# Moving a chain of small steps one to six places later in a hand-written order: layer 1's sums' stage of a two-layer graph attention kernel

## The chip, the cores and the metric

The kernel runs on one core of a Trainium2 chip, as one program. The metric is device time in microseconds (us), from one launch to its end. Three runs of the kernel before took 2566.87, 2554.59 and 2565.46 us; the median is 2565.46 us.

The core has a matrix engine (TensorE, PE in the profile; its weight loads are listed apart as PEld), a vector engine (VectorE, DVE), an engine for activations and copies (ScalarE, ACT), a general engine that here issues the gathers (GpSimd, POOL), and an engine that issues plain transfers (SyncE, SP). Each works through its own list of instructions in order. One waits for another by semaphores. PE writes to an accumulator memory (PSUM); the other operands lie in the on-chip memory (SBUF).

## The reference, cut to what matters

Two layers of relational graph attention over 3125 nodes of 768 features and 53125 edges (both directions and the loops) of three types, then a residual sum and a layer norm:

```python
def rgat_conv(x, W, q, k, b, src, dst, etype, heads, out_ch, n_nodes):
    xr = jnp.einsum('nd,rdf->rnf', x, W)
    oi = xr[etype, dst]; oj = xr[etype, src]
    alpha = jax.nn.leaky_relu(oi @ q + oj @ k, 0.2)
    m = jax.ops.segment_max(alpha, dst, num_segments=n_nodes)
    e = jnp.exp(alpha - m[dst])
    z = jax.ops.segment_sum(e, dst, num_segments=n_nodes)
    a = e / (z[dst] + 1e-16)
    msg = (a[:, :, None] * oj.reshape(-1, heads, out_ch)).reshape(-1, heads * out_ch)
    return jax.ops.segment_sum(msg, dst, num_segments=n_nodes) + b

h = jax.nn.elu(rgat_conv(x, W1, q1, k1, b1, ..., heads=4, out_ch=192))
out = rgat_conv(h, W2, q2, k2, b2, ..., heads=1, out_ch=768)
return layernorm(x + out)
```

Edges are sorted by `dst`. So the edges that end in one block of 128 nodes are one run of at most 17 slots of 128 edges.

## The kernel before, in words

There are 25 blocks of 128 nodes, and three stages after the set-up. Stage 1 (`phase1`) makes the table `x W1` for all types, with the keys, queries and weights of the edges. Stage 2 (`phase2`, L933 to L1203) is the one that changes. Stage 3 (`phase3`) gathers and sums for layer 2 and writes the output.

In stage 2 every block goes through five kinds of work:

1. **Gathers.** `gather(k)` (the helper at L490) has POOL issue one indirect transfer: 128 rows of 772 floats from the table into one of 14 buffers (`share` and `g`, `NG` at L937). There are 17 for a block, 14 for block 0.
2. **Selections.** `high(k)` (L1001, helper L482) has DVE make four matrices, one a head, that hold the edges' weights at the node of each edge.
3. **Sums.** `sums(k)` (L1010, matmuls at L1028): PE adds the selected rows into the accumulator `acc`. The 17 slots are taken in two batches of 96 matmuls, 128x32 by 128x193. A batch is issued when its last slot has come up: the first with the 8th slot of the block, the second with the 17th. A gather's buffer is free again when the sums that read it are done.
4. **The chain from the sums to the next layer's input.** `e_y` on DVE (L1036, L1037, and four L1041: divide by the sum of the weights and add the bias, result `y`), `e_x` on ACT (L1047: `ey = exp(y)`), `e_h` on DVE (L1087, L1088: ELU, in `ey`), `e_t` on PE (L1095: six 128x128 transposes into `pt`), `e_s` on ACT (L1102: the high part of `hT`) and `e_s2` on DVE (L1108: the low part). `y`, `ey` and `pt` have one buffer each, `hT` two.
5. **The dense products.** `d_part` (L1125, matmuls L1121): `h W2` in 18 parts of about 4.5 matmuls each, 90 in all (72 with 512 columns and 18 with 262). They write five pieces of the result into `po`, which has two buffers: pieces 0 to 3 take 18 matmuls of 512 columns each, piece 4 takes 18 of 262. `d_row(b, p)` (L1133) empties piece p: DVE copies two short columns of piece 0 (L1140, L1141) and one column into a row's start (L1145), ACT copies the rest (L1148) into the rows `r`, and SP stores a finished row into the table of layer 2 (L1153). So piece p+2 can't start before ACT has copied piece p.

What sets the order is written out by hand: a loop over steps k, one a slot of 17 a block (427 steps up to the last sums), and a list `ev` of what else is issued at a step. In a step the order is: the gather of slot k, the late keys, the sums of slot k-5, the selections of slot k-3, then what `ev` holds, older blocks first. No scheduler moves anything after that, so each engine's list is in this order. For block b, step e is the step after that of its second batch of sums:

```python
            e = SLF + i * SL + LAG          # one step after the block's last sums
            if i > 0:
                for d, f in ((0, e_y), (1, e_x), (2, e_h), (3, e_t), (4, e_s), (4, e_s2)):
                    when(e + d, f, b)
            e += 6
            for m in range(6 * R):
                k = e + m * SL // (6 * R) if i else first + 5 + m * (SL + 3) // (6 * R)
                when(k, d_part, b, m)
```

The products of a block so run over 17 steps, under the sums of the next block, and end beside that block's own chain. Block 0 has a chain of its own (`e_first`) and spreads its 18 parts over 20 steps.

Two things more stand in this order. The last four blocks (`LATE`) get the weights of their edges in this stage: four key gathers on POOL a block (`key`, L953) for 17 blocks (1 to 17), at step e+8, and four times the steps `l_load` to `l_put` (L956 to L996), which use the tiles `y`, `ey` and `pt` between two chains. And at step 427, SP issues the loads of `x` for stage 3 (`x_load3`).

Of the kernel before, what the change touches and what calls it, by code (L numbers as in the profile page):

```python
# [37 lines left out]
SL = 17  # L38
# [22 lines left out]
def kernel(  # L61
# [21 lines left out]
    R = layers[0]["W"].shape[0]  # L83
# [376 lines left out]
    def base(b):  # L460

        return SLF + (b - 1) * SL if b else 0
# [470 lines left out]
    def phase2(work, psum, wH, wL):  # L933
# [226 lines left out]
        def when(k, f, *a):  # L1160
            ev.setdefault(k, []).append((f, a))

        LAG = 5
        first = SLF + LAG - 1
        for i, b in enumerate(order):
            e = SLF + i * SL + LAG
            if i > 0:
                for d, f in ((0, e_y), (1, e_x), (2, e_h), (3, e_t), (4, e_s), (4, e_s2)):
                    when(e + d, f, b)
            e += 6  # L1170
            for m in range(6 * R):
                k = e + m * SL // (6 * R) if i else first + 5 + m * (SL + 3) // (6 * R)
                when(k, d_part, b, m)
                for p, (f, n) in enumerate(PIECES):
                    if m < (f + n) * 6 * R / WW <= m + 1:
                        when(k + 1, d_row, b, p)
            when(e + 2 + SL, d_q, b)
        at_key = {base(2 + i // KEYS) + 13: keys[i // KEYS * KEYS:i // KEYS * KEYS + KEYS]
                  for i in range(0, len(keys), KEYS)}
        for i in range(LATE):  # L1180
            e = base(2 + (SL * (i + 1) - 1) // KEYS + 2) + LAG
            for d, f in ((5, l_load), (6, l_alpha), (7, l_max), (8, l_scan), (10, l_back), (11, l_put)):
                when(e + d, f, NB - LATE + i)
        for k in range(max(ev) + 1):
            if k < NK:
# [359 lines left out]
    with tc.manual_schedule():  # L1545
        with tc.tile_pool(name="share", bufs=1) as pool:
# [4 lines left out]
            with tc.tile_pool(name="wbuf", bufs=1) as wbuf:  # L1551
# [33 lines left out]
                with tc.tile_pool(name="work2", bufs=1) as work, tc.tile_pool(name="psum2", bufs=1, space=PSUM) as psum:  # L1585
                    phase2(work, psum, wH, wL)
# [540 lines left out]
```

## Time and profile before

| what | us | from |
|---|---|---|
| median of three runs | 2565.46 | times |
| profiled execution, its own time | 2581.38 | times |
| its span, first to last instruction | 2579.6 | profile |
| stage 2: first sums to last dense product | 812.5 to 1803.3 | timeline |
| 17 blocks with key gathers (1 to 17), from the end of block 1's sums to that of block 18's | 692.3, or 40.7 a block | timeline |
| 6 blocks without (18 to 23), to the end of block 24's sums | 210.6, or 35.1 a block | timeline |
| from the end of block 24's sums to the last product | 27.2 | timeline |

The span is that of one profiled execution, on the same program; its own time of 2581.38 us stands 15.9 us (0.6%) above the median of the three runs. A block's time is counted from the recorded end of its second batch of sums to that of the next block. In a row of the timeline the first number is the start in us, the second the time taken, then engine, line, operation, output and inputs; in brackets stands the engine's idle time before it and what ended it ("remote" and "issue": nothing that the profile shows).

### The profile page before, as it was taken

What the parts mean: (1) busy time and instruction counts of PE and PEld (TensorE: products, weight loads), DVE (VectorE), ACT (ScalarE), POOL (GpSimd) and SP (SyncE); (2) the same over time, 40 slices, a digit from 0 to 9 for tenths busy, and PEclk for the clock granted to TensorE, in tenths of its full rate; (3) what the DMA queues carried; (4) which work ended last, traced back from release to release, by engine and by line L of the source; (5) the groups of instructions that cost most, each with busy time, mean ns of one, the idle gap of its engine ahead of it and who ended that gap; (6) DMA issues with size and microseconds to landing.
All of it is one profiled execution on the core that took longest, in us unless ns stands there. A gap on an engine that the chain in (4) does not pass through costs nothing.

```text
span 2579.6 us, 40091 instructions
## 1 busy us (share of the span) xinstructions
PE 1916.1 (74%) x13939; PEld 1341.8 (52%) x13939; DVE 1198.0 (46%) x4331; ACT 383.7 (15%) x834; POOL 1347.9 (52%) x1326
## 2 busy tenths in 40 slices
PE   8958887888996888788888888989365554455555
PEld 8846676666775666565655656667022222222223
DVE  7423443433544545455454555563244444445444
ACT  6301111111110111101111111111011111111111
POOL 4355666555533454555555455441655566556551
PEclk9978898888998888898989989999566666667667
DMA  7633343443568665665656657665867777767772
GB/s 224 154 114 109 126 150 112 139 135 111 183 211 297 191 210 177 199 187 186 215 176 207 192 191 237 213 220 171 286 212 239 252 262 269 252 226 252 242 236 84
DMA packets 161766, 506.39 MB, mean 196 GB/s; under 512 B 48028, under 2 KB 57521, under 8 KB 161556
## 3 DMA queue, kind: packets, MB, share of 16 engines
q0 software_dynamic: 81936, 331.52, 41.5%
q1 hardware_dynamic: 69389, 157.78, 17.5%
q10 hardware_dynamic: 10230, 14.43, 1.7%
q8 instruction: 114, 1.87, 0.3%
q14 instruction: 97, 0.79, 0.1%
HBM read 412.74 MB, written 95.69 MB: 197 GB/s over the span
## 4 chain that ended last, share of the span: by engine, by line
PE 22%; another core or an unknown queue 18%; issue 15%; DVE 10%; POOL 6%; ACT 2%; DMA 1%; POOLq 0%; ACTq 0%; DVEq 0%; SPq 0%
PE po L1121 8%; POOL G L490 6%; DVE selp L482 5%; PE acc L1340 5%; PE po L742 4%; PE acc L1028 3%; DMA G<-ftab,ridx 1%; ACT r L1148 1%; DVE sT L1251 1%; PE pt L1095 1%; ACT hT L1102 1%; DVE y L1041 0%; ACT ey L1047 0%; DVE F L1299 0%
## 5 line engine op out<-in xcount | busy, mean ns | idle before, releaser
L1121 PE MATMUL po<-wH,hT 128*128 128x512 f32 (+1 forms) x1500 | 487.9, 409 | 61.1 <-ACT hT L1102 58.3
L490 POOL DMA_INDIRECT kt<-kt,ridx x374 | 396.6, 1060 | 248.2 <-issue 108.5
L490 POOL DMA_INDIRECT G<-ftab,ridx x374 | 377.9, 1010 | 276.3 <-PE acc L1340 115.9
L742 PE MATMUL po<-wH,xT 128*128 128x512 f32 (+1 forms) x1320 | 433.8, 404 | 39.1 <-ACT share L774 17.8
L1340 PE MATMUL acc<-G,selp 128*32 128x385 f32 (+1 forms) x2292 | 304.6, 637 | 165.6 <-issue 91.7
L482 DVE TENSOR_SCALAR selp<-frow,fdl,pall 128x32 f32<-128x32 f32 (+1 forms) x1688 | 376.3, 313 | 9.7 <-remote 9.7
L490 POOL DMA_INDIRECT share<-ftab,ridx x239 | 247.4, 1035 | 244.9 <-PE acc L1028 162.7
L1121 PEld LDWEIGHTS po<-wH,hT 128*128 128x128 f32 x1500 | 301.8, 212 | 135.1 <-ACT hT L1102 62.0
L742 PEld LDWEIGHTS po<-wH,xT 128*128 128x128 f32 x1320 | 258.6, 205 | 102.1 <-issue 30.2
L1121 PE MATMUL po<-wL,hT 128*128 128x512 f32 (+1 forms) x750 | 308.1, 411 | 0.0
L1340 PEld LDWEIGHTS acc<-G,selp 128*32 128x32 f32 x2292 | 128.1, 134 | 315.8 <-issue 194.6
L742 PE MATMUL po<-wL,xT 128*128 128x512 f32 (+1 forms) x660 | 260.2, 394 | 8.6 <-issue 8.1
L490 POOL DMA_INDIRECT g<-ftab,ridx x135 | 139.9, 1036 | 148.4 <-PE acc L1028 99.7
L1028 PE MATMUL acc<-share,selp 128*32 128x193 f32 x3088 | 198.9, 340 | 23.7 <-issue 14.1
L1148 ACT COPY r<-po 128x262 f32<-128x262 f32 (+5 forms) x175 | 71.8, 436 | 737.1 <-remote 391.0
L1121 PEld LDWEIGHTS po<-wL,hT 128*128 128x128 f32 x750 | 160.2, 214 | 33.9 <-issue 7.7
L1028 PEld LDWEIGHTS acc<-share,selp 128*32 128x32 f32 x3088 | 119.5, 113 | 89.2 <-issue 60.0
L742 PEld LDWEIGHTS po<-wL,xT 128*128 128x128 f32 x660 | 135.2, 205 | 34.3 <-issue 12.2
L1251 DVE TENSOR_SCALAR sT<-bc,cols 128x512 bf16<-128x512 f32 (+1 forms) x125 | 82.8, 662 | 94.5 <-PE bc L1245 91.8
L1028 PE MATMUL acc<-g,selp 128*32 128x193 f32 x1688 | 119.4, 334 | 5.7 <-issue 5.4
L1245 PE MATMUL bc<-d,one 1*128 1x512 bf16 (+1 forms) x125 | 49.4, 395 | 95.6 <-DVE sT L1251 67.3
L1271 DVE TENSOR_TENSOR oh<-oh,pq 128x153 f32<-128x153 f32 x25 | 7.9, 316 | 213.9 <-remote 200.6
(309 smaller groups left out, 2040.9 us busy)
## 6 DMA issues: line engine op xcount, KB each, us to landing
ftab<-r SPq DMA_DIRECT2D x74, 386.0 KB
ftab<-share SPq DMA_DIRECT2D x71, 386.0 KB
share<-in_L_gnn_W_dram SPq DMA_DIRECT2D x36, 384.0 KB
w_d<-w2hl SPq DMA_DIRECT2D x18, 768.0 KB
sT<-dr_d SPq DMA_DIRECT2D x25, 534.0 KB
share<-in_x_dram SPq DMA_DIRECT2D x27, 384.0 KB
xb_d<-share SPq DMA_DIRECT2D x25, 384.0 KB
xr<-in_x_dram SPq DMA_DIRECT2D x21, 384.0 KB
```

The source lines that it names most:

```text
L482: V.tensor_scalar(sel.rearrange("p (t f) -> p t f", f=32), of, dl[:, b, j:j + 1], p, op0=ALU.is_equal, op1=ALU.mult)
L490: return G.indirect_dma_start(out=to, out_offset=None, in_=tab, in_offset=_index(i[:, j:j + 1]), bounds_check=NP * R - 1, oob_is_err=False)
L742: m = T.matmul(po[:, :n], xT[:, s, t, :], w[:, t, KQ + f:KQ + f + n], start=(i == 0), stop=(i == 3 * DT - 1))
L1028: T.matmul(acc[32 * t:32 * t + 32, h // 2, c], sel[:, h, 32 * WINDOW[i].index(t):][:, :32], g[:, h * CW:(h + 1) * CW], start=(i == u[0] an ...
L1095: T.transpose(pt[:, t // 3, (t % 3) * P:(t % 3 + 1) * P], s["ey"][:, t * P:(t + 1) * P], ident)
L1102: S.copy(hT[:, 0], p3)
L1121: T.matmul(po[:, :n], hT[:, k, t, :], w[:, t, f:f + n], start=(i == 0), stop=(i == 3 * DT - 1))
L1148: S.copy(o[:, 1 + at - a:1 + at + m], po[:, got - a:got + m])
L1245: T.matmul(bc[:, :n], one, s["d"][:, 4 * i * P:4 * i * P + n], start=True, stop=True)
L1251: V.tensor_scalar(s["sT"][:, 4 * i * P:4 * i * P + n], bc[:, :n], cols[:, b:b + 1], None, op0=ALU.is_equal)
L1271: V.tensor_mul(oh, oh, s["pq"][:, :SL * R * 3].rearrange("p (j k) -> p j k", j=SL))
L1340: T.matmul(acc[32 * t:32 * t + 32, c, :HALF + c], st[b, j][:, 32 * WINDOW[j].index(t):][:, :32], gs[:, (base(b) + j) % NG, 1 + c * HALF:][ ...
```

## The change

The chain's steps move: `e_y`, `e_x` and `e_h` by one step, `e_t` by three, `e_s` and `e_s2` by four. The dense products of every block but block 0 move by six steps (and the `d_row` and `d_q` with them); block 0's keep their start and are spread over 26 steps. The late blocks' steps `l_load` to `l_put` move by two to five. What is computed, the buffers and the number of instructions stay the same.

```diff
             e = SLF + i * SL + LAG
             if i > 0:
-                for d, f in ((0, e_y), (1, e_x), (2, e_h), (3, e_t), (4, e_s), (4, e_s2)):
+                for d, f in ((1, e_y), (2, e_x), (3, e_h), (6, e_t), (8, e_s), (8, e_s2)):
                     when(e + d, f, b)
-            e += 6
+            e += 12
             for m in range(6 * R):
-                k = e + m * SL // (6 * R) if i else first + 5 + m * (SL + 3) // (6 * R)
+                k = e + m * SL // (6 * R) if i else first + 5 + m * (SL + 9) // (6 * R)
                 when(k, d_part, b, m)
...
-            for d, f in ((5, l_load), (6, l_alpha), (7, l_max), (8, l_scan), (10, l_back), (11, l_put)):
+            for d, f in ((8, l_load), (9, l_alpha), (9, l_max), (12, l_scan), (13, l_back), (16, l_put)):
                 when(e + d, f, NB - LATE + i)
```

In PE's list of a block this reads as follows. Before: second sums of block b, 23 matmuls of products of block b-1, the six transposes of b, the last 17 products of b-1, the first 10 of b, first sums of b+1, 40 products of b, second sums of b+1. After: second sums of b, 36 products of b-1, the transposes of b, first sums of b+1, the last 31 products of b-1 (13 of 512 columns and 18 of 262), the first 23 of b, second sums of b+1.

In ACT's list, before: the copy of piece 2 of block b-1, exp of b, piece 3, high part of `hT` of b, piece 4. After: the two copies of piece 1 of block b-1, exp of b, piece 2, high part of `hT` of b, piece 3, piece 4.

## The prediction

> **What bounds the kernel now.** First I read stage 2's share and the waits in it, then one block's timeline on PE, DVE, ACT and POOL. The waits name two stalls of PE, and both are in the chain that the change moves:
>
> ```profile
> PE pt L1095 <- DVE ey L1088: 63.2, 23, 3.0
> ...
> PE po L1121 <- ACT hT L1102: 58.3, 17, 5.0
> ```
>
> The first is the transposes' wait for `ey`, 2.75 us in each of 23 blocks; the second the next products' wait for `hT`, 3.4 us in 17 blocks. The table by stretches, from the end of block 1's sums to that of block 18's and of block 24's:
>
> ```profile
> 873.17:1565.43 692.26, 576.34 (x4909) 421.38 (x4909) 345.90 (x1486) 76.22 (x156) 367.89 (x358) 0.89 0.62 194
> 1565.43:1776.07 210.64, 190.25 (x1733) 144.95 (x1733) 119.32 (x512) 26.65 (x55) 97.48 (x95) 0.94 0.66 210
> ```
>
> Columns: time, then busy time of PE, PEld, DVE, ACT, POOL, the granted clock, DMA share, GB/s. PE is busy 83 and 90% of the time, no other engine over 57%, DMA 62 to 66%: PE sets the pace. Its clock is 0.89 and 0.94 of full speed; the difference to 1 is lost too. One block with key gathers:
>
> ```profile
> 1323.58 0.68 PE L1028 MATMUL acc<-share,selp 128*32 128x193 f32 x9 [0.21 <-issue]
> ...
> 1332.54 0.88 PE L1095 MATMUL pt<-fident,ey 128*128 128x128 f32 x6 [2.84 <-DVE ey L1088]
> ```
> ```profile
> 1327.43 0.16 DVE L1036 TENSOR_SCALAR rz<-acc 128x4 f32<-128x4 f32 x1 [6.07 <-remote]
> ...
> 1331.53 0.96 DVE L1088 SCALAR_TENSOR_TENSOR ey<-y,ey 128x768 f32<-128x768 f32 x1
> ```
> ```profile
> 1328.20 0.59 ACT L1148 COPY r<-po 128x512 f32<-128x512 f32 x1 [11.72 <-remote]
> 1329.35 0.84 ACT L1047 ACTIVATE ey<-y 128x768 f32<-128x768 f32 x1 [0.56 <-issue]
> 1335.49 0.66 ACT L1148 COPY r<-po 128x6 f32<-128x6 f32 x2 [5.29 <-remote]
> 1338.96 0.80 ACT L1102 CAST hT<-pt 128x768 fp32r<-128x768 f32 x1 [2.81 <-remote]
> ```
>
> Read them against each other. PE's sums end at 1324.26, but DVE sees them at 1327.43, 3.2 us later. The last matmul of piece 2 ends at 1325.39 and ACT's copy starts at 1328.20 (2.8 late); piece 3's ends at 1329.58 and its copy starts at 1335.49 (5.9 late); the transposes end at 1333.42 and `hT` starts at 1338.96 (5.5 late). Why PE's results arrive late isn't shown ("remote"), but it goes with POOL's runs of gathers. In this block POOL issues without a pause, the four keys last:
>
> ```profile
> 1323.84 1.00 POOL L490 DMA_INDIRECT share<-ftab,ridx  x1 [0.72 <-remote]
> ...
> 1337.58 1.00 POOL L490 DMA_INDIRECT kt<-kt,ridx  x1 [0.30 <-issue]
> ```
>
> `hT` comes 0.4 us after this run ends at 1338.58. In the first block without keys the run ends at 1574.55, and `hT` follows its transposes at once:
>
> ```profile
> 1575.79 0.81 ACT L1102 CAST hT<-pt 128x768 fp32r<-128x768 f32 x1
> ```
>
> In block 24, with no gathers left, the sums end at 1776.07 and DVE starts 0.1 us later:
>
> ```profile
> 1776.16 0.16 DVE L1036 TENSOR_SCALAR rz<-acc 128x4 f32<-128x4 f32 x1 [7.18 <-PE acc L1028]
> ```
>
> So a block costs 40.7 us with keys and 35.1 without. Free of both stalls and at full clock the first would be 40.7 - 3.4 - 2.75 - 0.11 x 40.7 = 30.1 us, the second 35.1 - 2.75 - 0.06 x 35.1 = 30.2. Both give the same floor, 30.2.
>
> **The change part by part.** No instruction is added or removed. I count from the recorded end of block b's second sums (time 0); 512-column products come every 0.238 us (23 in 5.5).
>
> *Transposes.* PE now reaches them after 36 products, at 36 x 0.238 = 8.6 instead of 5.4. `ey` is ready at 3.2 + 5.1 = 8.3 in the block above. That alone would end the stall. But ACT's exp now stands behind the two copies of piece 1, whose last matmul is the 13th after the sums: it ends at 13 x 0.238 + 0.2 = 3.3. Its lateness in a run of gathers isn't in the trace. Below, it is 0.1 (block 24) or, with gathers, 2.8 (piece 2, ending at 1.1); above, 5.9 (piece 3, ending at 5.3). I take 3.9, nearer the first, which it follows by 2.2 us. Copies start at 7.2 and take 0.65; exp starts at 8.0 and takes 0.85; L1087 and L1088 take 1.6: transposes at 10.5. Stall 1.9 us instead of 2.75 (ends: 0.8 with 2.8, 3.9 with 5.9).
>
> *hT.* Between the transposes and block b's first product PE now has the first sums of b+1 (5.4 us in this block) and 31 products (13 x 0.238 + 18 x 0.122 = 5.3): 10.7 us. `hT` is 5.5 late at worst here, its two parts take 1.8: the stall of 3.4 goes. If the run of gathers goes on through the next batch's, 10.7 may just not cover it; then up to 3 us come back.
>
> *Pieces.* Piece 3 starts after 31 products, at 7.4, and needs piece 1's copies, done at 7.9: 0.5, inside the 1.9 above. Piece 0 of b starts 2.2 us after piece 3 ends; its copies are 0.7 and lateness after first sums was 0.65 to 3.5 (L1140, 1269.39 to 1270.05 and 1310.78 to 1313.95). A stall of 0 to 2; I take 0.5.
>
> *Clock.* Blocks without keys have one gap of 2.75 us and lose 2.1 us of clock; those with keys have two and lose 4.5. For one gap of 1.9 I take 1.5 (ends 0 and 4.5).
>
> The block: 30.2 + 1.9 + 0.5 + 1.5 = 34.1 us. 17 x (40.7 - 34.1) = 112, and 6 x (35.1 - 34.1) = 6, so 118 us.
>
> *DVE and POOL.* DVE's lists shift by a step; it is busy 57% of 35 us, and the 8 slots' selections for the first sums (0.9 us a slot) are done by about 12.5, when PE still has half of that batch before it. POOL's list doesn't change: 17 gathers and 4 keys, 21 x 1.305 = 27.4 us of 34.1. The first sums come 5 us sooner after the second ones, but their last rows are issued before time 3. The rows 14 to 16 are issued behind the keys, at 14.6 to 18.5, and are needed at about 28. DMA: 194 GB/s x 40.7 us = 7.9 MB a block; in 34.1 us that is 232 GB/s, and the slices of the page reach 262 to 297.
>
> *Late steps.* `l_scan` stands on DVE three steps behind `l_max` instead of one, so DVE's wait (27.4 us in four) gets shorter or stays; they are four blocks. Nothing, bounds -4 and +4 us.
>
> *Both ends of the stage.* After block 24's sums PE has 31 parts instead of 25: 27.2 + 6 x 1.1 = 33.8, 6.6 more. At the front the same products are missing: nine matmuls before block 1's sums and four parts in the next block, 2.2 + 4.3 = 6.5 us less, if rows are there in time. SP's queue: the stores of block 23's rows now stand behind the eleven loads at step 427 (4.2 MB, some 19 us at 220 GB/s), and block 24's copies into the same rows wait for them; they are needed at 19 to 27. I take +2 in all, bounds -2 and +12.
>
> **Sum:** -118 + 2 = -116 us, counted on the profiled execution's 2581.4 (2465). It stands 15.9 above the median, so for the median 2565.5 - 116 = 2449 us.
>
> **The rivals.** *Full clock.* The gap of 1.9 is too short to lower the clock: block 32.6, 17 x 8.1 + 6 x 2.5 - 2 = 151, 2415 us. Against it: gaps of 2.85 us cost clock in block 18, where the transposes ran at half pace (1.54 us for six, 0.88 in the block above):
>
> ```profile
> 1573.73 1.54 PE L1095 MATMUL pt<-fident,ey 128*128 128x128 f32 x6 [2.85 <-DVE ey L1088]
> ```
>
> The Trainium skill, page TensorE: Matmul & The Clock Gate, section Why this matters for your kernels, says that only idle gaps over about 3 us drop the clock; by that rule this rival would be right, and the trace with its 2.85 stands just outside it.
>
> *No stall at all:* lateness of 1.5 or less. Block 30.2: 17 x 10.5 + 6 x 4.9 - 2 = 206, 2360. Against it: 2.8 is the least seen with gathers at that place, and POOL and DMA have no slack left at that pace.
>
> *Gathers or po buffers hold it:* block 36, as 35.1 is what the blocks without keys take now: 17 x 4.7 - 6 x 0.9 - 2 = 73, 2493.
>
> *Slower: exp behind the copies.* If piece 1's end reaches ACT only when POOL's run is through, as `hT` did, at 9.7 without keys and 11.8 with (piece 3's copies: 9.8; 11.2 to 12.6), the transposes start 3.2 later, at 12.9 and 15.0. Stalls 4.3 and 6.4, clock 3 and 4.5, piece 0.5: blocks of 38.0 and 41.6. 17 x 0.9 + 6 x 2.9 + 2 = 35 slower: 2600. It decides from a start of the copies near 10.9. For it: results after piece 2's were always late to the run's end; against it: piece 1 ends 2 us before piece 3 did.
>
> *Nothing gained:* between these two, 2565.
>
> **How the numbers follow.** Forecast 0.42 (2449, own range 2425 to 2480), full clock 0.18, no stall 0.12, held at 36 0.11, slower 0.12, no change 0.05. The range of 2375 to 2555 leaves out the slower rival, most of "no stall" and half of "no change". A measurement of this kernel can tell about 0.5% (13 us) from no change. Faster 0.42 + 0.18 + 0.12 + 0.11 = 0.83, same 0.05, slower 0.12.
>
> **What would show it.** The wait of the products for `hT` (58.3 us) gone; that of the transposes down from 63 to about 45; ACT's exp starting right behind two copies of 262 and 250 columns, 8 us after the sums; a granted clock of about 0.95 in blocks 1 to 23; 34 us a block with and without keys alike; 34 us from the last sums to the last product. Wrong would make it: exp 11 us or more after the sums, a new wait of products for ACT's copies over 2 us a block, or sums waiting for gathered rows.

## The result, and the profile after

The changed kernel took a median of 2536.15 us (2528.77 to 2541.26, four runs), the kernel before beside it 2566.16 us (2554.59 to 2580.24, four runs). The ratio is 0.9869, with a 95% interval of 0.9822 to 0.9916: 1.3% faster, 30 us where 116 were forecast. A second set of runs gave 0.9856 (0.9798 to 0.9915).

The profiled execution of the changed kernel took 2528.77 us (span 2527.0). The stage, from the first sums to the last product, went from 990.8 to 923.1 us. First the table of waits of the whole kernel (columns: total us, times, longest); these answer to the two lines that named the stalls before:

```profile
PE acc L1028 <- issue: 50.3, 118, 1.1
...
PE po L1121 <- ACT r L1148: 17.2, 6, 3.7
...
PE po L1121 <- remote: 8.9, 3, 3.0
...
PE pt L1095 <- issue: 6.1, 6, 2.4
...
PE pt L1095 <- DVE ey L1088: 2.7, 3, 0.9
```

The products' wait for `hT` (58.3 us) is gone, and the transposes' wait fell from 63.2 us to 2.7 and 6.1. What took their place stands above them: products that wait for ACT's copies out of `po` (17.2 and 8.9), and PE's idle time inside the sums, with nothing named that ends it. That is 50.3 us now; in the same table of the kernel before it was 19.5:

```profile
PE acc L1028 <- issue: 19.5, 76, 1.1
```

The table by stretches, from the end of block 1's sums to that of block 18's and of block 24's (time, busy time of PE, PEld, DVE, ACT, POOL, then granted clock, DMA share, GB/s):

```profile
891.06:1530.40 639.34, 563.60 (x4892) 420.98 (x4891) 348.22 (x1485) 75.07 (x154) 360.52 (x359) 0.93 0.67 210
1530.40:1720.89 190.49, 182.06 (x1733) 135.74 (x1733) 118.11 (x508) 26.78 (x55) 94.32 (x94) 1.00 0.74 232
```

That is 37.6 us a block with key gathers (40.7 before, 34.1 forecast) and 31.7 without (35.1 before, 34.1 forecast). So the blocks without keys did better than forecast, and those with keys fell short.

One block with keys, whose second sums end at 1005.43. PE's timeline (start, time taken, engine, line, operation, in brackets the idle time before it):

```profile
1014.12 0.87 PE L1095 MATMUL pt<-fident,ey 128*128 128x128 f32 x6
1014.91 1.68 PE L1028 MATMUL acc<-g,selp 128*32 128x193 f32 x21
1016.96 0.32 PE L1028 MATMUL acc<-g,selp 128*32 128x193 f32 x1 [0.37 <-issue]
1017.68 0.34 PE L1028 MATMUL acc<-g,selp 128*32 128x193 f32 x1 [0.40 <-issue]
1019.08 0.54 PE L1028 MATMUL acc<-g,selp 128*32 128x193 f32 x2 [1.06 <-issue]
1020.51 0.60 PE L1028 MATMUL acc<-g,selp 128*32 128x193 f32 x4 [0.89 <-issue]
```

POOL's timeline in the same block:

```profile
1009.07 1.00 POOL L490 DMA_INDIRECT share<-ftab,ridx  x1 [1.23 <-PE po L1121]
...
1012.98 1.00 POOL L490 DMA_INDIRECT g<-ftab,ridx  x1 [0.30 <-issue]
1014.29 1.00 POOL L490 DMA_INDIRECT kt<-kt,ridx  x1 [0.30 <-issue]
...
1018.20 1.00 POOL L490 DMA_INDIRECT kt<-kt,ridx  x1 [0.30 <-issue]
1021.65 1.00 POOL L490 DMA_INDIRECT g<-ftab,ridx  x1 [2.45 <-PE acc L1028]
```

And ACT's:

```profile
1009.78 0.65 ACT L1148 COPY r<-po 128x262 f32<-128x262 f32 x2 [10.03 <-PE po L1121]
1010.80 0.84 ACT L1047 ACTIVATE ey<-y 128x768 f32<-128x768 f32 x1 [0.38 <-issue]
...
1020.60 0.80 ACT L1102 CAST hT<-pt 128x768 fp32r<-128x768 f32 x1 [3.70 <-remote]
```

In this block the exp comes 5.4 us after the sums, the transposes don't wait at all, and the first sums begin at once behind them. After 21 matmuls they go on singly or in twos, 0.7 us or more apart instead of 0.05, until 1020.5. POOL issues the four keys from 1014.29 to 1019.20, so this falls on the second half of the keys and the 1.3 us behind them. Neither rows nor selections explain it: POOL had issued the eight gathers of these sums by 1005.2, and DVE had finished their last selection at 1015.8, ahead of the first gap (when a row lands isn't recorded). From 1019.13 to 1025.96 the granted clock is 0.50, so the matmuls that follow are slow as well, and the 96 end 11.4 us after they began. `hT` is again 5.6 us late and starts 1.4 us after the last key gather ends at 1019.20, but nothing waits for it now. So the change does what it says; the run of gathers that used to delay `hT` now falls on the first sums.

### The profile page after: what moved, and what is told of

Read it like the earlier page. It is cut to its first block, busy times and chain, and to the rows that moved or that the text cites. A ratio compares the mean times of both kernels' runs of the same rounds, so it can differ in the third digit from the quotient of the medians.

```text
span 2527.0 us, 40133 instructions
## 1 busy us (share of the span) xinstructions
PE 1899.4 (75%) x13939; PEld 1335.0 (53%) x13939; DVE 1199.7 (47%) x4331; ACT 383.1 (15%) x834; POOL 1332.5 (53%) x1326
## 4 chain that ended last, share of the span: by engine, by line
PE 51%; issue 20%; another core or an unknown queue 9%; POOL 8%; DVE 7%; DMA 2%; ACT 1%; POOLq 0%; DVEq 0%; SPq 0%; ACTq 0%
PE po L1121 17%; PE po L742 16%; PE acc L1028 9%; POOL G L490 7%; PE acc L1340 3%; DVE selp L482 2%; PE bank L299 1%; DMA G<-ftab,ridx 1%; PE pt L277 1%; PE pt L1095 1%; PE po L414 1%; PE px L714 1%; DVE sT L1251 0%; PE pq L649 0%
## 5 line engine op out<-in xcount | busy, mean ns | idle before, releaser
L1121 PE MATMUL po<-wH,hT 128*128 128x512 f32 (+1 forms) x1500 | 449.9, 384 | 32.4 <-ACT r L1148 17.2
L742 PE MATMUL po<-wH,xT 128*128 128x512 f32 (+1 forms) x1320 | 431.6, 403 | 46.5 <-issue 34.3
L1340 PE MATMUL acc<-G,selp 128*32 128x384 f32 (+1 forms) x2292 | 303.8, 635 | 162.6 <-issue 88.9
L482 DVE TENSOR_SCALAR selp<-frow,fdl,pall 128x32 f32<-128x32 f32 (+1 forms) x1688 | 380.6, 316 | 31.7 <-remote 26.4
L490 POOL DMA_INDIRECT share<-ftab,ridx x239 | 239.9, 1004 | 206.1 <-PE acc L1028 125.4
L1121 PEld LDWEIGHTS po<-wH,hT 128*128 128x128 f32 x1500 | 274.4, 192 | 107.6 <-issue 37.4
L1121 PE MATMUL po<-wL,hT 128*128 128x512 f32 (+1 forms) x750 | 285.4, 381 | 0.5 <-issue 0.2
L1028 PE MATMUL acc<-share,selp 128*32 128x193 f32 x3088 | 229.5, 363 | 46.0 <-issue 35.2
L1028 PEld LDWEIGHTS acc<-share,selp 128*32 128x32 f32 x3088 | 144.0, 120 | 109.2 <-issue 87.3
L1121 PEld LDWEIGHTS po<-wL,hT 128*128 128x128 f32 x750 | 144.4, 193 | 28.4 <-issue 2.0
L742 PEld LDWEIGHTS po<-wL,xT 128*128 128x128 f32 x660 | 134.3, 203 | 39.3 <-issue 16.5
L1028 PE MATMUL acc<-g,selp 128*32 128x193 f32 x1688 | 134.3, 350 | 15.8 <-issue 15.1
L1028 PEld LDWEIGHTS acc<-g,selp 128*32 128x32 f32 x1688 | 82.6, 116 | 48.5 <-issue 38.6
```

Of the source, the lines that this page charges most:

```text
L482: V.tensor_scalar(sel.rearrange("p (t f) -> p t f", f=32), of, dl[:, b, j:j + 1], p, op0=ALU.is_equal, op1=ALU.mult)
L490: return G.indirect_dma_start(out=to, out_offset=None, in_=tab, in_offset=_index(i[:, j:j + 1]), bounds_check=NP * R - 1, oob_is_err=False)
L742: m = T.matmul(po[:, :n], xT[:, s, t, :], w[:, t, KQ + f:KQ + f + n], start=(i == 0), stop=(i == 3 * DT - 1))
L1028: T.matmul(acc[32 * t:32 * t + 32, h // 2, c], sel[:, h, 32 * WINDOW[i].index(t):][:, :32], g[:, h * CW:(h + 1) * CW], start=(i == u[0] an ...
L1121: T.matmul(po[:, :n], hT[:, k, t, :], w[:, t, f:f + n], start=(i == 0), stop=(i == 3 * DT - 1))
L1340: T.matmul(acc[32 * t:32 * t + 32, c, :HALF + c], st[b, j][:, 32 * WINDOW[j].index(t):][:, :32], gs[:, (base(b) + j) % NG, 1 + c * HALF:][ ...
```

## The experiments

The whole kernel's time turned out a poor witness: in 18 profiles the code ahead of the stage, the same in all of them but for some clears of buffers in the run with short rows, took between 794.5 and 832.7 us. So the runs are compared by the stage (first sums to last product), by its blocks, and by the length of their first 96 matmuls of sums, all worked out from the recorded starts and ends on the timeline. Each figure is that of one profiled execution. The three profiles of the kernel before differ by up to 16 us in the stage, so a difference of that size between two rows shows nothing. Where no ratio is given below, the kernel was executed once.

| run | stage | block 1 to 17 | block 18 to 23 | first sums, 1 to 17 | second sums, 1 to 17 |
|---|---|---|---|---|---|
| before, three profiles | 990.8, 977.1, 974.4 | 40.7, 40.2, 39.8 | 35.1, 34.4, 35.1 | 5.4 (first) | 5.2 |
| changed, two profiles | 923.1, 926.3 | 37.6, 37.6 | 31.7, 32.3 | 9.3, 8.6 | 5.3, 5.2 |
| changed, no keys | 885.0 | 34.1 | 35.3 | 5.7 | 5.2 |
| changed, keys early | 920.4 | 36.7 | 33.0 | 5.6 | 7.5 |
| before, keys early | 969.1 | 39.2 | 35.0 | 5.1 | 8.9 |
| earlier exp | 920.5 | 37.7 | 31.2 | 10.2 | 5.3 |
| earlier exp, no keys | 846.4 | 32.9 | 32.6 | 5.6 | 5.3 |
| same, POOL clears tiles instead | 864.8 | 33.9 | 32.5 | 4.5 | 5.7 |
| earlier exp, short rows | 968.2 | 38.8 | 36.2 | 8.0 | 9.1 |
| products alone moved | 1006.2 | 39.9 | 39.3 | 5.7 | 5.2 |
| earlier exp, pauses | 900.1 | 36.8 | 30.7 | 4.7 | 5.4 |
| earlier exp, pauses, keys split | 861.8 | 34.3 | 31.3 | 5.2 | 6.6 |
| before, pauses | 898.3 | 35.9 | 33.8 | 7.8 | 5.3 |
| before, pauses, keys split | 894.0 | 35.4 | 34.3 | 5.5 | 6.8 |
| changed, pauses, keys split | 861.7 | 34.5 | 30.6 | 5.3 | 6.9 |

**The keys: left out, and moved.** The first question was whether the key gathers make the 6 us between the two kinds of block.

```diff
-            for i in at_key.get(k, ()):
-                key(*i)
```

> The changed kernel without the 68 key gathers (17 steps of four); the last four blocks get wrong weights, nothing else is left out. In the changed kernel a block with keys takes 37.6 us and one without 31.7. Theory K (the keys' place: they are issued while PE works on the first sums, whose matmuls then come one by one): blocks 1 to 17 fall to about 31.7, 100 us less in the profile. Theory V (volume: 21 gathers a block, wherever they stand, keep POOL and PE's results late): the same here. Theory C (the copies of piece 1 that stand ahead of the exp are what costs): the blocks stay above 36, under 30 us less.

Measured: 34.1 us in blocks 1 to 17, about halfway between 37.6 and 31.7. The first sums are back at 5.7 us, as theories K and V have it. Most blocks took 29 to 35 us, but four of the 17 took 42 to 43, and two of the six after them as well. That second kind is looked at below.

```diff
-        at_key = {base(2 + i // KEYS) + 13: keys[i // KEYS * KEYS:i // KEYS * KEYS + KEYS]
+        at_key = {base(2 + i // KEYS) + 4: keys[i // KEYS * KEYS:i // KEYS * KEYS + KEYS]
```

> The changed kernel with each step of four key gathers nine steps earlier, behind the gather of slot 4 instead of slot 13, where POOL waits for the second sums. Nothing is left out. Theory K: blocks 1 to 17 fall from 37.6 to 32 or 33 us, 80 to 95 us faster (ratio to the kernel before about 0.955). Theory V and theory C: no change against the changed kernel (ratio about 0.987).

Measured: 2517.15 us, ratio 0.983 (0.9744 to 0.9915), the stage 920.4 us against 923.1. The first sums are whole again (5.6 us), but now the second sums take 7.5 us. The keys cost where they fall: theory V is nearer than K. The stages are too close to be told apart.

> The kernel before with the same move of the keys alone. Theory K: the products' wait for hT (3.4 us in 17 blocks) goes without the change's later products, blocks 1 to 17 fall from 40.7 to 35 to 37 us, 60 to 95 us faster than the kernel before (ratio 0.963 to 0.977): more than the whole change brought. Theory V: no change, ratio 1.00.

Measured: ratio 0.9977 (0.9936 to 1.0019); its stage took 969.1 us, 5 to 22 less than the three profiles of before (its profiled execution, 2588.24 us, was the longest of its ten). The second sums went from 5.2 to 8.9 us and gave back what the `hT` stall had cost. K was wrong here.

**The copies ahead of the exp.**

```diff
-                for d, f in ((1, e_y), (2, e_x), (3, e_h), (6, e_t), (8, e_s), (8, e_s2)):
+                for d, f in ((0, e_y), (1, e_x), (2, e_h), (6, e_t), (8, e_s), (8, e_s2)):
```

> The changed kernel with y, exp and ELU one step earlier again (as before the change), so that ACT's exp stands ahead of the two copies of piece 1; transposes, hT and products stay late. Theory C: exp starts 5 us or less after DVE has the sums in every block, the transposes' wait goes in the 8 blocks that still have it, 30 to 50 us faster than the changed kernel (ratio to the kernel before 0.97). Theory K: under 15 us either way (ratio 0.982 to 0.992), as piece 3 then waits up to 0.9 us longer for piece 1's copies.

Measured: 2499.71 us, ratio 0.9776 (0.9689 to 0.9862). That looks like theory C, but the stage took 920.5 us, 3 less than in the changed kernel; the rest is the unchanged code ahead of it, 794.6 us in this profile. Exp comes 1.8 to 1.9 us after DVE has the sums in every block, so the late exps are gone; in their place the first sums take 10.2 us. Theory C named the late exps rightly and falls for the size of it in the stage; the ratio's interval overlaps with that of the changed kernel.

**Both taken away, and the keys replaced by other work.** The earlier exp together with no keys; then the same with 24 clears of a 68-column tile on POOL in the keys' place.

```diff
-                key(*i)
+                for _ in range(6):
+                    G.memset(kts[i[0] % 2], 0.0)
```

> The changed kernel with y, exp and ELU a step earlier, and without the 68 key gathers (wrong weights in the last four blocks, nothing else left out). With the keys the earlier exp gave 37.7 us in blocks 1 to 17 and 31.2 in 18 to 23. If keys and a late exp are the two causes of what a block takes over 31 us, nearly all of the 23 blocks take 30 to 32 us and none 40 or more: the stage about 870 us from first sums to last product. If the blocks of 40 to 43 us have a third cause, several of them stay.

> As the run before, but in the keys' place POOL clears a small tile 24 times, an estimated 4 to 5 us of plain work without transfers (wrong weights in the last four blocks). Theory E (a POOL without a pause is what delays, whatever it does, or the later gathers behind it): hT 5 us late again, first sums one by one, blocks 1 to 17 at 37 us. Theory P or B (it takes gathers): hT within 1.3 us of its transposes, blocks at 31.

Measured: 32.9 and 33.9 us in blocks 1 to 17, where 30 to 32 and 31 were expected. Theory E falls. In the second run POOL is as busy as with the keys, and the first sums don't suffer (4.5 us); `hT` starts within 1.3 us of its transposes in 22 of the 23 blocks. POOL's timeline in one block, then PE's, then ACT's:

```profile
959.74 1.00 POOL L490 DMA_INDIRECT g<-ftab,ridx  x1 [0.30 <-issue]
960.73 5.11 POOL L1189 MEMSET kt<- 128x68 f32 x24
966.47 1.01 POOL L490 DMA_INDIRECT g<-ftab,ridx  x1 [0.63 <-PE acc L1028]
```
```profile
960.87 0.87 PE L1095 MATMUL pt<-fident,ey 128*128 128x128 f32 x6 [0.18 <-DVE ey L1088]
961.67 1.52 PE L1028 MATMUL acc<-g,selp 128*32 128x193 f32 x32
963.01 2.81 PE L1028 MATMUL acc<-share,selp 128*32 128x193 f32 x64
```
```profile
961.64 0.59 ACT L1148 COPY r<-po 128x512 f32<-128x512 f32 x1 [2.70 <-remote]
962.12 0.80 ACT L1102 CAST hT<-pt 128x768 fp32r<-128x768 f32 x1
```

The 96 matmuls run through in 4.2 us under POOL's clears, and `hT` follows 0.4 us after the transposes, behind piece 2's copy. It takes gathers to delay them.

Blocks of 38 to 42 us stay in the run with the earlier exp and no keys: 4 of 23. These are the third cause, and the changed kernel shows it too. In each of the four the products stop for 3.4 to 3.7 us until ACT copies out of `po`, behind a run of six gathers. The block whose sums end at 925.80 took 42.9 us; ACT's rows, then PE's, then POOL's:

```profile
935.49 0.65 ACT L1148 COPY r<-po 128x262 f32<-128x262 f32 x2 [14.91 <-remote]
936.02 0.86 ACT L1047 ACTIVATE ey<-y 128x768 f32<-128x768 f32 x1
...
954.84 0.94 ACT L1148 COPY r<-po 128x6 f32<-128x6 f32 x3 [12.25 <-remote]
```
```profile
955.55 0.80 PE L1121 MATMUL po<-wH,hT 128*128 128x512 f32 x1 [3.46 <-ACT r L1148]
```
```profile
951.35 1.00 POOL L490 DMA_INDIRECT g<-ftab,ridx  x1 [0.30 <-issue]
952.66 1.01 POOL L490 DMA_INDIRECT g<-ftab,ridx  x1 [0.31 <-issue]
```

Piece 1's last matmul ended 3.2 us after the sums, its copies start 6.5 us after that. Later the copies of the last pieces start at 954.84, 1.2 us after POOL's last gather of that run ends at 953.67; the products of the next block had been waiting for them for 3.46 us, and go on at a lower clock (0.50 from 954.24 to 961.06).

**Bytes or issues.** The kernel with the earlier exp, and the row gathers of the stage with 64 of 772 columns.

```diff
-            gather_rows(gs[k % NG], tab1, *in_turn(k))
+            gather_rows(gs[k % NG][:, :64], tab1, *in_turn(k))
```

> The changed kernel with the earlier exp and with its keys, but the row gathers of this stage bring 64 of 772 columns, a twelfth of the bytes; the other columns of the buffers are ones, so the result is wrong. POOL's issues are as many and as long. Theory P (issuing gathers on POOL holds back what PE reports): DVE still sees the sums 3 to 4 us late, hT is 5 us late, first sums one by one, blocks 1 to 17 at 36 to 38 us. Theory B (the bytes in flight do it): sums seen within 0.5 us, hT within 1.3, blocks at 30 to 31.

Measured: neither. In blocks 2 to 23 DVE sees the sums 1.0 to 1.7 us after their end (theory B's direction), yet the blocks take 38.8 and 36.2 us. In the two fences below, PE's timeline and then POOL's (two lines are added to this kernel ahead of them, so L1030 is the sums' L1028): now row gathers, with a twelfth of the bytes, are issued while the sums run, and the sums again come in ones and threes.

```profile
970.01 3.17 PE L1030 MATMUL acc<-g,selp 128*32 128x193 f32 x65
...
973.57 0.54 PE L1030 MATMUL acc<-share,selp 128*32 128x193 f32 x3 [0.22 <-issue]
974.32 0.34 PE L1030 MATMUL acc<-share,selp 128*32 128x193 f32 x1 [0.21 <-issue]
...
976.46 0.44 PE L1030 MATMUL acc<-share,selp 128*32 128x193 f32 x3 [1.04 <-issue]
```
```profile
970.82 0.99 POOL L490 DMA_INDIRECT g<-ftab,ridx  x1 [2.32 <-PE acc L1030]
...
974.71 1.00 POOL L490 DMA_INDIRECT g<-ftab,ridx  x1 [0.30 <-issue]
976.93 0.99 POOL L490 DMA_INDIRECT g<-ftab,ridx  x1 [1.22 <-remote]
```

So gathers break up the sums with few bytes as well, and short rows do it as well as keys. With fewer bytes PE's results do arrive sooner.

That POOL issues gathers isn't enough, though. POOL issues full rows at the same pace of one in 1.3 us, and they hardly do it: in the changed kernel a matmul of the sums comes every 0.06 us on average while POOL issues rows, and every 0.16 us while it issues keys. In the changed kernel without keys, with runs of up to nine full rows, PE has no unexplained gap of 0.3 us or more ahead of sums or products in blocks 1 to 23; with the keys it has 48 such gaps, 31 us in all. Every gather has 128 rows, of 16 bytes for keys, 256 for short rows and 3088 for full ones. Whether it is the small pieces, or what a run of them does to the gathers behind them, no run here separates.

**One part of the change alone.** Products and late steps moved, the chain at its old steps.

```diff
-                for d, f in ((1, e_y), (2, e_x), (3, e_h), (6, e_t), (8, e_s), (8, e_s2)):
+                for d, f in ((0, e_y), (1, e_x), (2, e_h), (3, e_t), (4, e_s), (4, e_s2)):
```

> One part of the change alone: the dense products and the late blocks' steps as changed, the chain from y to hT at the steps it had before. The transposes come up some 20 products (4.8 us) after the sums: their wait for the ELU of 2.5 to 3 us in each of 23 blocks stays, that for hT goes. If the parts add up, blocks 1 to 17 take 37 to 38 us as in the changed kernel (the chain's move only buys 1 us a block), blocks 18 to 23 take 35; the stage 940 to 950 us from first sums to last product, against 991 before and 923 changed.

Measured: 39.9 and 39.3 us, the stage 1006.2 us, where 940 to 950 were expected. This is 15 to 32 us slower than before, and about 80 us slower than the whole change. The waits of the whole kernel:

```profile
PE pt L1095 <- DVE ey L1088: 73.1, 23, 4.8
...
PE po L1121 <- ACT r L1148: 60.0, 19, 3.8
```

The stall for `hT` is gone, as expected; in 19 places products wait for ACT's copies instead. The parts don't add up: in this one execution the products' move doesn't pay without the later transposes. The chain's move alone was not run.

**The changed kernel again, and pauses on POOL.** If PE's results get through when POOL stops issuing gathers, stopping it on purpose should help. The pause is plain work of 1.3 us, behind the gathers of slots 8 and 0 and ahead of the keys.

```diff
+        junk = work.tile([P, 56], F32, name="junk", bufs=1)
+
+        def pause():
+            for _ in range(6):
+                G.memset(junk, 0.0)
...
             gather_rows(gs[k % NG], tab1, *in_turn(k))
+            if k >= SLF and (k - SLF) % SL in (8, 0):
+                pause()
...
+            if k in at_key:
+                pause()
             for i in at_key.get(k, ()):
```

> The changed kernel once more, unchanged, beside the next three. In the first pair of profiles the stage that the change touches took 67.7 us less (990.8 to 923.1 from first sums to last product), but the unchanged stage ahead of it 18.9 us more. If that was chance, this profile's stage is within 10 us of 923 and the stage ahead anywhere from 795 to 831; if the change did it, the stage ahead takes 825 or more again.

Measured: 2530.88 us, ratio 0.9856 (0.9798 to 0.9915), the stage 926.3 us and the code ahead of it 827.0.

> The changed kernel with the earlier exp, and with POOL doing 1.3 us of plain work (six clears of a small tile) behind the gathers of slots 8 and 0 of every block and ahead of each step of four keys; nothing is left out. Theory P (PE's completions get through when POOL stops issuing gathers for about a us): DVE sees the sums and ACT the pieces earlier, the blocks of 40 us or more go, first sums lose less than now; blocks 1 to 17 take 33 to 35 us instead of 37.7, though POOL has 4 us more to do in each; ratio to the kernel before about 0.955. Theory B (the bytes under way hold PE back): the pauses bring nothing, blocks 37 to 39, ratio 0.975 to 0.99.

Measured: 2487.24 us, ratio 0.9701 (0.9638 to 0.9764). The blocks without keys fall to 30.7 us, near the forecast's floor of 30.2, and the first sums are whole at 4.7 us although POOL begins the keys under them, right behind a pause; but the blocks with keys still take 36.8 us, where 33 to 35 were expected. What is broken up now are the products behind the sums: in the block below POOL issues keys from 994.0 and four rows behind them until 1004.2, and PE's unexplained gaps lie between 999.2 and 1005.5, in the second half of that run and behind it. PE's timeline of one block, where L1129 is the products' L1121:

```profile
999.76 0.42 PE L1129 MATMUL po<-wH,hT 128*128 128x262 f32 x2 [0.58 <-issue]
...
1001.22 0.40 PE L1129 MATMUL po<-wH,hT 128*128 128x262 f32 x2 [0.93 <-issue]
```

```diff
-        at_key = {base(2 + i // KEYS) + 13: keys[i // KEYS * KEYS:i // KEYS * KEYS + KEYS]
-                  for i in range(0, len(keys), KEYS)}
+        at_key = {base(2 + i // KEYS) + (21 if i % KEYS else 13): keys[i:i + 2]
+                  for i in range(0, len(keys), 2)}
```

> As the run before, but of the four keys of a step two stay behind slot 13 and two go behind slot 4 of the next block, with a pause ahead of each pair. Theory P: the run of gathers under the first sums is 2.6 us shorter, blocks 1 to 17 take 32 to 34 us, ratio to the kernel before about 0.95. If keys cost the same wherever they are, no better than the run before.

Measured: 2466.6 us, ratio 0.9606 (0.9552 to 0.966), blocks of 34.3 and 31.3 us. The keys cost less in pairs, two of them in another place.

> The kernel before with the same pauses of POOL (behind slots 8 and 0, ahead of the keys) and nothing else. Theory P: the wait of the transposes (63 us in 23 blocks) and that of the products for hT (58 us in 17 blocks) both shrink by half or more, blocks 1 to 17 fall from 40.7 to 36 to 38 us. Theory B: waits and blocks stay, or the blocks get longer by POOL's extra work.

Measured: 2496.38 us, blocks of 35.9 and 33.8 us, the stage 898.3. Pauses alone, which add work and move nothing, take more out of the kernel before than the whole change did (76 to 93 us of the stage, against 48 to 68). In its waits the one for `hT` is gone; what stays is the transposes' (63.2 before; L1103 is L1095 here):

```profile
PE pt L1103 <- DVE ey L1096: 49.2, 23, 2.2
```

Half of what theory P expected of the waits held: `hT` yes, the transposes by a fifth only, since DVE still sees the sums 2.5 us after their end instead of 3.2.

**Before twice more, and the change with and without its moves.**

> The kernel before, unchanged, for a second profile of its stages. If its first profile was typical, the stage from first sums to last product takes 985 to 995 us again and the change's 65 us there are real, and the stages around it must give back some 30 us. If it was untypically long, this one takes 960 to 975.

> The kernel before, unchanged, for a third profile. The same two readings as for the second; the spread of the three says how far a single profile's stage can be trusted.

Measured: stages of 977.1 and 974.4 us, the first had 990.8; the code ahead of it took 830.4 and 799.6 us, the first 812.5. So the first profile of before was long by 14 to 16 us in the stage, and the change's gain there is 56 us (mean of three, 980.8, less mean of two, 924.7).

> The kernel before with POOL's three pauses and the keys split in two pairs, and none of the change's moves. With four keys in one step the pauses gave 35.9 us in blocks 1 to 17 and 33.8 in 18 to 23. If the split helps here as it did in the changed order, blocks 1 to 17 fall to 34, the stage to 930 to 940 us, ratio to the kernel before 0.965 to 0.975. If the reordering is worth something of its own, this stays 15 us or more behind the same edits on the changed kernel (ratio 0.96).

> The changed kernel with the pauses and the split keys, but with y, exp and ELU where the change put them, the exp behind piece 1's two copies. If the place of the exp doesn't matter once pieces arrive early, blocks 1 to 17 take 34 to 34.5 us and the ratio is 0.96 as with the earlier exp (34.3 us, 0.961). If it does, the transposes wait 1 to 2 us in every block, which then takes 36, ratio 0.97.

Measured: ratio 0.9671 (0.9579 to 0.9762) for the kernel before with both edits, 0.9566 (0.9487 to 0.9645) for the changed kernel with them (2465.71 us). The stages took 894.0 and 861.7 us, and the medians 2497.69 and 2465.71 us: with late results out of the way, the reordering is still worth 32 us, though the two intervals overlap. On the kernel before the split did little: 35.4 us in blocks 1 to 17, where 34 was expected. The place of the exp doesn't matter any more. The table by stretches of the last run, columns as above:

```profile
890.55:1477.67 587.12, 534.21 (x4892) 396.41 (x4891) 347.78 (x1485) 75.81 (x154) 421.64 (x766) 0.99 0.71 229
1477.67:1661.27 183.60, 179.61 (x1733) 138.18 (x1733) 118.63 (x508) 27.26 (x55) 104.69 (x161) 1.00 0.74 240
```

The granted clock is 0.99 and 1.00. This kernel and the one with the earlier exp are the fastest here, about 4% under the kernel before, and can't be told apart.

## Why the prediction was wrong

The sign was right and the size was not: 1.3% where 4.5% was forecast. The time lies in the range given, between the rivals "held at 36" and "nothing gained". The step that failed is *DVE and POOL*: POOL's unchanged list of gathers was costed at nothing, and it cost 3.9 us in the first sums of each of 17 blocks. In the profiled stage the blocks with keys fell 3.5 us short each (60 us), those without did 2.4 us better (14 us), and the two ends took 3 us more than forecast: that makes the 48 us between the forecast's 116 and the 67.7 measured there. The working compared a block's terms; here they stand beside the measured ones, in us a block. PE's idle time is summed by what it stood ahead of, and clock is the time lost to a clock below full speed.

| term | before, 1 to 17 | forecast, all | changed, 1 to 17 | changed, 18 to 23 |
|---|---|---|---|---|
| ahead of transposes | 2.9 | 1.9 | 0.4 | 0.3 |
| ahead of products | 3.6 | 0.5 | 1.7 | 0.6 |
| inside the sums | 0.4 | in the floor | 2.3 | 0.5 |
| clock | 4.6 | 1.5 | 2.6 | 0.0 |
| the rest | 29.3 | 30.2 | 30.5 | 30.3 |
| block | 40.7 | 34.1 | 37.6 | 31.7 |

- *Transposes.* The stall shrank, by more than forecast: 0.4 us is left, not 1.9. The lateness of piece 1's copies was taken as 3.9 us, between two rows. In the changed kernel it is never that: of the 22 blocks 2 to 23, 14 have 0.4 to 1.5 us and 8 have 5.0 to 6.5. A value between two groups described no block. Only in the 8 late ones does PE stand still there, the products first. The rival "exp behind the copies" comes near to what happens in those 8 (copies start up to 9.7 us after the sums; it was to hold from 10.9).
- *hT.* Right. The stall of 3.4 us went, the results are as late as ever (5.6 us in the block shown), and 10.7 us of cover held.
- *Pieces.* 0.5 forecast, 1.7 measured, but 1.0 of it stands ahead of the transposes, where the forecast counted it into its 1.9. The two stalls together took 2.1 us against 2.4, which is luck: they come in some blocks only, the products' in single waits of 1.4 to 3.7 us, where a run of gathers outlasts PE's lead of two pieces. The lateness quoted as up to 3.5 was 3.2 by its own rows.
- *DVE and POOL* is the step that failed: "POOL's list doesn't change", with 27.4 us of 34.1, was costed at nothing because no row came late. The first sums were carried over at 5.4 us. They took 9.3, 3.9 us more in 17 blocks, or 66 us. Of the 3.9 us, 1.9 are idle time between the matmuls and 1.3 a lower clock. In the kernel before, the keys didn't lie under the sums: PE stood in the `hT` stall during the last of them and the 2 us behind, and the first sums began 6 us behind the run (1344.5 against 1338.6 in the block of the prediction). So their price for PE's own work couldn't be seen there; the change laid the first sums over them. The experiments without keys (5.7 us) and with clears in their place (4.5) show that it is theirs; the early keys show that it moves with them to the second sums (7.5 us).
- *Clock.* 0.93 and 1.00, forecast "about 0.95". The rule weighed there was the Trainium skill's, page TensorE: Matmul & The Clock Gate, section Why this matters for your kernels: it says to leave no idle gaps over about 3 us, as one window of idle drops the clock. By that rule gaps of 2.4 us are harmless; in the run without keys a single gap of 2.39 us was followed by transposes at half pace, so the trace disagrees. Behind gaps of 1.7 and 0.9 us, the changed kernel's transposes kept 0.87 us. But several short gaps close together lower the clock too: in the block shown the clock is 0.50 right behind three gaps of 0.37, 0.40 and 1.06 us. Of the 2.6 us a block, some 1.0 is lost in or behind the broken first sums.

```profile
896.26 1.54 PE L1095 MATMUL pt<-fident,ey 128*128 128x128 f32 x6 [2.39 <-issue]
```

- *Late steps and both ends.* The tail took 33.5 us, forecast 33.8. The front saved 1.0 us instead of 6.5: 60.7 before, 59.7 after.
- *The blocks alike, 34 us with keys and without.* Wrong: 37.6 and 31.7. That blocks differ by what POOL issues was in the rows quoted (the run "the four keys last"), but it was read as a cause of late results alone.
- *From the profile to the median.* The sum was made against a profiled execution whose stage was 14 to 16 us longer than in two later ones. Of the 56 us that the stage gains by the means, 30 and 37 arrived at the medians. In the two profiles of the changed kernel the unchanged code ahead of the stage took 831.3 and 827.0 us, in the three of before 812.5, 830.4 and 799.6. Other kernels with the same code there had 794.5 to 832.7, so this looks like chance; two profiles don't exclude that the change has a part in it, and it stays open.

What stays open as well is why these gathers slow PE. The runs show when they do, and that many bytes aren't needed and a POOL busy with plain work isn't enough; none of them shows the path that the two share.

## What to carry to other kernels

When a stall is taken away, ask what was going on during it that cost nothing: here four gathers on another engine, free while PE stood still, and 3.9 us of PE's time when it didn't. A result that is "late" by an amount that changes from row to row should be read against what the other engines do at that moment; if it has two modes, forecast the two and their shares, not a value between them. A long unbroken run of gathers can be worth breaking up: pauses of 1.3 us took more off this stage (76 to 93 us, in one execution) than the reordering (48 to 68), at no cost in instructions on the engine that set the pace.

## What the runs showed of the hardware

- Late in a run of gathers that has keys or short rows in it, and for about 1.3 us behind it, PE's matmuls of the sums, and the products too, come 0.7 us apart or more, with nothing in the trace that they wait for. The start of such a run behind a pause doesn't do it (with the pauses, a matmul of the sums comes every 0.05 us while POOL issues keys), runs of full rows alone hardly do, and clearing tiles on POOL doesn't (96 matmuls in 4.2 us).
- PE's results mostly reach ACT and DVE about 1.1 us after POOL's last gather of a run. With the earlier exp, DVE saw the sums 1.1 or 1.2 us after the end of a gather in 21 of 23 blocks, and `hT` came 1.2 to 1.5 us after the last key in 16 of 17. In 9 blocks of the changed kernel the sums were seen after 3.0 to 3.3 us while a run went on. With rows of 64 columns they were seen after 1.0 to 1.7 us instead of 3.0 to 4.0.
- A single idle gap of 2.39 us on PE was enough to lower its clock, and so were three gaps of 0.37, 0.40 and 1.06 us within 2.5 us (0.50 for the 6.8 us behind them).
- The same code ahead of the stage (with some clears added in one run) took 794.5 to 832.7 us in 18 profiles, a spread of 4.7%: a change of 1% in this kernel is better read from its stage than from its total.
